# A two-layer scan kernel: old y added where y is copied out, and the second layer's preparation and stores spread over steps

## The chip, the cores and the metric

The kernel runs on one core of one Trainium2 chip. The metric is device time in microseconds (us) of one execution. Four engines compute: TensorE (PE: matrix products and transposes, into PSUM), VectorE (DVE), ScalarE (ACT) and GpSimd (POOL). SyncE (SP) issues most transfers, POOL issues those that add into memory. [...]

## The reference, cut to what matters

Two residual layers work on a picture of 4 batches x 64 x 64 positions x 192 channels. Each normalises its input, projects it to 384 inner channels and a gate, and runs a state-space scan with 16 states over the 4,096 positions in four directions: by rows, by columns, and both backwards. The four results are added, normalised, gated, and projected back.

```python
# first layer: a recurrence along L for each of 4 directions
dA = jnp.exp(dt[..., None] * A_k[None])
dBu = dt[..., None] * bt[:, :, None, :] * ut[..., None]
h = dA * h + dBu
y = jnp.einsum('bkdn,bkn->bkd', h, ct)
...
y = out_y[:, 0] + inv_y[:, 0] + wh_y + invwh_y
# second layer: the same kind of sum, by cumulative sums with a decay
log_decay = jnp.cumsum(log_dA, axis=1)
decay = jnp.exp(log_decay)
h = decay * jnp.cumsum(dB_u / (decay + 1e-12), axis=1)
y = jnp.einsum('bldn,bln->bld', h, C_mat)
```

In the second layer the decay dies out after a few positions for most states, so the kernel computes only the positions near the ends of each direction (and keeps a full version for data where that does not hold, behind a runtime test; it is not run on this data).

## The kernel before, in words

**First layer** (class FirstLayer, once per batch). `project` writes the transposed input uT, the skip term as the first value of y, and the B, C and dt rows to device memory. `scans` then works on 32 items, each one direction and 512 positions: items 0 to 15 go by rows (forward and backward in turn), 16 to 31 by columns. An item has 16 steps, one per state, numbered n; g numbers all 512 steps. In a step:

- ACT makes `xT` (L699, for step g+2) and the decay `a` (L711, for g+1);
- PE transposes xT into PSUM tiles `x` (L716, for g+1), of which there are three;
- DVE scans `h` along the positions in three pieces (L724) and keeps the last column (`carry`, L734);
- POOL multiplies `h` by the C row, broadcast over partitions by SP (`bct`, L704, L738);
- PE, at least three steps later (LAG = 3), transposes the product and adds it into three PSUM banks `yp` (`add_y`, L751).

The old y of the item's positions is loaded as `yold` (one SBUF buffer). PE puts it into `yp` by a product with the identity (`start_y`, L745) at steps 3 and 4, so that the sums begin from it; the item's own sums are added from step 4 on. `end_y` (L764) copies the banks to `yt` at steps 2 and 3 of the next item and SP stores it. For items that go the same way (rows or columns) as the one before, `yold` is loaded at step 5 of the item before. For item 16, the first by columns, it is loaded only after the last store by rows (L838).

Between these run the preparations of later items (`steps`, L668), each put at a step by hand: dt products on PE, Abs, Exp and Ln on ACT, four instructions on POOL, sums on DVE. The order on PE, ACT, DVE and POOL in this stage is the one written (a manual schedule); SP follows in the order of the program.

**Second layer** (class SecondLayer, all four batches in turn within each stage). `project`, then `prepare`, `scans` and `finish`. `prepare` takes two chunks per batch, main (M) and extension (E). For each it loads `uc`, makes the B, C and dt rows (`xp`, L1234), then in `delta` dt products (`dp`, L1160; three PSUM banks), Abs (L1167), Exp (L1168), four POOL instructions (L1171, L1172, L1173, L1175), Ln (L1174), the dt products once more and their use on DVE (L1177); then cumulative sums, a test, a product with uc (L1241), and in `keep` transposes and five stores. This part has no order written by hand: the framework's planner orders each engine's instructions by what is ready and by their place in the program.

`scans` of the second layer is written by hand again, with 9 steps per batch: four on M, two on a half-width chunk (two states each), one on E, two on a quarter-width chunk (four states each). For each step ACT makes a weight `sg` and a decay `a` (L1296), one step ahead; for the steps with four states POOL first multiplies (L1285) and ACT then takes one function of the whole (L1291). DVE multiplies and scans (L1344, L989), POOL multiplies by C (L1360), PE adds up two steps later (L1378). Results go to memory through transfers that add (`store`, L1407), issued by POOL: per batch six for the E result `yte` and six for the sum `ytm`, all six in a row. `store` takes four blocks; the first and third are one transfer each (L1412), the second and fourth two (L1415).

Of the kernel before, what the change touches and what calls it, by code (L numbers as in the profile page):

```python
# [10 lines left out]
F32 = mybir.dt.float32  # L11
# [6 lines left out]
ND = DI // 128  # L18
# [384 lines left out]
class FirstLayer:  # L403
# [151 lines left out]
    def scans(self):  # L555
        nc, tc = self.tc.nc, self.tc
        with ExitStack() as ctx:
# [181 lines left out]

            def start_y(it, b):  # L740

                if b == 0:
                    it.yp = [ps_y.tile([128, LC], F32, name=f"yp{i}") for i in range(ND)]
                yo = it.yold.rearrange("p j e -> p (j e)")[:, b * LC : (b + 1) * LC]
                nc.tensor.matmul(it.yp[b], ident, yo, start=True, stop=False, skip_group_check=True)  # L745

            def add_y(g, b):
                it, n = flat[g]
                for i in range(NJ):
                    j, d = divmod(b * NJ + i, ND)  # L750
                    nc.tensor.matmul(  # L751
                        it.yp[b][:, i * 128 : (i + 1) * 128],
                        hs[g][:, d, j * 128 : (j + 1) * 128],
                        ident,
                        start=False,
                        stop=n == NS - 1,
                        is_transpose=True,
                        skip_group_check=True,
                    )
# [21 lines left out]
            with tc.manual_schedule(engines={nc.tensor.engine, nc.scalar.engine, nc.vector.engine, nc.gpsimd.engine}):  # L781
# [17 lines left out]

                items[0].yold = load("yold", self.y_dram, items[0].k, items[0].c)  # L800
                c_rows(0)
# [7 lines left out]
                for g in range(N + LAG + 1):  # L809
# [10 lines left out]
                    adds = [[] for _ in range(ND)]  # L820
                    if it is not None:
                        for at, b in (((LAG, 1), 0), ((LAG, 2), 1), ((LAG + 1, 0), 2)):
                            if at[0] == n:
                                adds[at[1]].append((start_y, it, b))

# [4 lines left out]
                    for d in range(ND):  # L830
# [12 lines left out]
                    if g < N:  # L843
# [148 lines left out]
class SecondLayer(FirstLayer):  # L992
# [149 lines left out]
    def prepare(self, ucs, batches):  # L1142
        nc, tc = self.tc.nc, self.tc
        with ExitStack() as ctx:
# [17 lines left out]

            def delta(xd):

                e = p3.tile([128, ND, LC], F32, name="e")
                for d in range(ND):
# [8 lines left out]
                nc.gpsimd.tensor_tensor(e, e, wl, ALU.add)  # L1175
                for d in range(ND):
                    nc.vector.scalar_tensor_tensor(dt[:, d, :], dt_rows(xd, d), 0.0, e[:, d, :], ALU.max, ALU.add)  # L1177
                return dt, e

# [46 lines left out]

            for uc_dram, (main, ext, _, _) in zip(ucs, batches):
                before = None
                for r, chunk in enumerate((main, ext)):
                    uc = p2.tile([128, ND, LC], F32, name="uc")  # L1230
                    nc.sync.dma_start(uc, uc_dram[:, r])
                    xp = ps_x.tile([NX, LC], F32, name="xp")
                    for d in range(ND):
                        nc.tensor.matmul(xp, self.w_xp[:, d, 0, :], uc[:, d, :], start=(d == 0), stop=(d == ND - 1))  # L1234
                    xd = p2.tile([NX, LC], F32, name="xd")
                    nc.scalar.activation(xd, xp, AF.Identity, bias=self.xbias)
                    dt, e = delta(xd)
                    cum = sums(dt, before)
                    before = cum
                    test(cum, r)  # L1240
                    nc.vector.tensor_mul(e, dt, uc)  # L1241
                    if r == 0:
                        for at in (0, SEG, 3 * SEG - 1, 4 * SEG - 1):
                            nc.vector.memset(dt[:, :, at : at + 1], 1e30)
                    keep(chunk, xd, dt, cum, e)


    def scans(self, batches, ys):
        nc, tc = self.tc.nc, self.tc
        with ExitStack() as ctx:  # L1250
            pool = lambda name, bufs, **k: ctx.enter_context(tc.tile_pool(name=name, bufs=bufs, **k))
            p1, p2, p3, p5 = (pool(f"s{b}", b) for b in (1, 2, 3, 5))
            ps_y = pool("psy", 1, space=bass.MemoryType.PSUM)
# [134 lines left out]
            def ext_y(g, b):  # L1388
# [8 lines left out]
                if b == ND - 1:  # L1397
                    store(it.y, flat[g][2], SEG)

            def end_y(b):  # L1400
                y = p1.tile([128, NJ, DI], F32, name="ytm")
                for i in range(ND):
                    to = y.rearrange("p j e -> p (j e)")[:, i * LC : (i + 1) * LC]
                    (nc.scalar.copy if i == 1 else nc.vector.tensor_copy)(to, yp[i])
                store(y, b, 0)

            def store(y, b, near):  # L1407
                far = near + SEG
                v = ys[b].rearrange("(h w) e -> w h e", w=HW)
                for k, lo in enumerate((near, near, L - far, L - far)):  # L1410
                    if k % 2 == 0:
                        nc.gpsimd.dma_start(ys[b][lo : lo + SEG, :], y[:, k, :], accum_op=ALU.add)  # L1412
                        continue
                    for s in range(2):
                        nc.gpsimd.dma_start(v[lo // HW + s], y[s * HW : (s + 1) * HW, k, :], accum_op=ALU.add)  # L1415

            with tc.manual_schedule(engines={nc.tensor.engine, nc.scalar.engine, nc.vector.engine, nc.gpsimd.engine}):
# [12 lines left out]
                for g in range(N + LAG + 1):  # L1430
# [30 lines left out]

# [127 lines left out]
```

## Time and profile before

| | us |
|---|---|
| median of 3 runs | 11277.36 |
| lowest to highest of them | 11272.01 to 11278.86 |
| the profiled execution's own time | 11280.24 |
| its span, first to last instruction | 11278.4 |

| engine | busy us | share of the span |
|---|---|---|
| PE | 9593.1 | 85% |
| DVE | 9659.2 | 86% |
| ACT | 9787.2 | 87% |
| POOL | 8583.8 | 76% |

The first layer's scans fill most of the span: about 200 to 2400 us for the first batch, and the same again from about 2670, 5140 and 7610 us. The second layer starts at about 9810 us; its preparation lies between 10456 and 10656 us, its scans between 10673 and 11024, its last stage after that.

Times inside the profile are us from the start of the span. A row of the groups gives line, engine, operation, output and inputs with their shapes, the count, and then the busy time with the mean ns of one, and the idle time just before with what ended it. A row of the waits gives who waited for whom, the total in us, how often, and the longest. A row of windows gives from:to and length in us, then for PE, its weight loads, DVE, ACT and POOL the busy us (and number of instructions), the granted TensorE clock as a share of full speed, the DMA share and GB/s. A row of the timeline gives start, length, engine, line and operation, and in brackets the idle time before it with what ended it. In shapes, f32 is 4 bytes; one fp32 product shows as two matmuls.

### The profile page before, as it was taken

The page shows a single profiled execution, that of the slowest core. Times are in us where ns is not written, and L with a number is a line of the kernel's source. Part 1 is how long each engine was busy: PE and PEld are TensorE (multiplying, and loading weights), DVE is VectorE, ACT ScalarE, POOL GpSimd, SP SyncE. Part 2 cuts the span into 40 slices and gives each one's busy share as a digit, 9 for nine tenths or more (in the row PEclk, how much of TensorE's full clock was granted, in tenths as well). Part 3 has the DMA queues.
Part 4 walks back from the last instruction along what each step waited for, and adds up shares of the span by engine and source line. Part 5 has one row for each costly group of instructions (what it writes and reads, how often), then busy time and mean ns, then how long its engine had stood idle before and what let it go on. Part 6 is the DMA issues. An engine that isn't in the chain of part 4 may idle for free. (4 is left out here: it accounts for less than half of the span.)

```text
span 11278.4 us, 171696 instructions
## 1 busy us (share of the span) xinstructions
PE 9593.1 (85%) x61449; PEld 7301.6 (65%) x61449; DVE 9659.2 (86%) x11524; ACT 9787.2 (87%) x16986; POOL 8583.8 (76%) x2776
## 2 busy tenths in 40 slices
PE   7998888878988888888988888879988888788667
PEld 4776666655776666656766666647766666655356
DVE  4999899976999899957999899939998999888465
ACT  5999999977999999958999999949999999856567
POOL 3999899945999899928999899909998999700360
PEclk8999999988999999988999999979999999989688
DMA  4333333444333333344333334343333333434448
GB/s 124 109 105 98 94 98 100 97 133 125 109 104 99 94 99 98 97 149 112 111 100 96 96 98 98 89 164 107 109 100 94 98 98 98 127 114 128 159 104 272
DMA packets 831026, 1269.85 MB, mean 113 GB/s; under 512 B 99002, under 2 KB 514631, under 8 KB 829652
## 3 DMA queue, kind: packets, MB, share of 16 engines
q1 hardware_dynamic: 825300, 1252.49, 39.6%
q0 software_dynamic: 4864, 6.29, 0.4%
q8 instruction: 488, 8.00, 0.3%
q14 instruction: 374, 3.06, 0.1%
HBM read 958.19 MB, written 300.42 MB: 112 GB/s over the span
## 5 line engine op out<-in xcount | busy, mean ns | idle before, releaser
L738 POOL TENSOR_TENSOR h<-h,bct 128x1536 f32<-128x1536 f32 x2048 | 7062.4, 3469 | 591.4 <-DVE carry L734 487.9
L724 DVE TENSOR_TENSOR_SCAN h<-a,carry,x 128x512 f32<-128x512 f32 x5376 | 6607.0, 1267 | 238.7 <-PE x L716 191.7
L716 PE MATMUL x<-ident,xT 128*128 128x128 f32 x24576 | 4002.0, 287 | 817.7 <-DVE h L724 715.7
L699 ACT ACTIVATE xT<-dtuT,bT 128x384 f32<-128x384 f32 x8192 | 4358.6, 609 | 94.8 <-PE x L716 90.1
L716 PEld LDWEIGHTS x<-ident,xT 128*128 128x128 f32 x24576 | 2805.6, 145 | 2142.7 <-DVE h L724 925.7
L711 ACT ACTIVATE a<-dt,A_log_f 128x512 f32<-128x512 f32 x6144 | 3977.5, 716 | 0.0
L751 PE MATMUL yp<-ident,h 128*128 128x128 f32 x24576 | 3705.5, 277 | 9.2 <-POOL h L738 9.2
L751 PEld LDWEIGHTS yp<-ident,h 128*128 128x128 f32 x24576 | 2946.5, 144 | 78.8 <-issue 64.1
L615 PE MATMUL dp<-xd,w_dtb_f 13*128 13x512 f32 x1536 | 886.9, 661 | 213.6 <-DVE dt L644 212.0
L724 DVE TENSOR_TENSOR_SCAN h<-a,x 128x512 f32<-128x512 f32 x768 | 899.1, 1207 | 190.0 <-PE x L716 115.7
L628 POOL TENSOR_SCALAR wl<-e 128x1536 f32<-128x1536 f32 x128 | 189.1, 1478 | 919.6 <-ACT e L624 919.6
L490 PE MATMUL pp<-xT,w_in 96*128 96x512 f32 x1152 | 535.3, 615 | 0.0
L615 PEld LDWEIGHTS dp<-xd,w_dtb_f 13*128 13x128 f32 x1536 | 237.3, 190 | 457.0 <-DVE dt L644 341.2
L745 PE MATMUL yp<-yold,ident 128*128 128x512 f32 x768 | 444.1, 663 | 73.4 <-DMA yold<-y 73.4
L621 ACT ACTIVATE e<-dp 128x512 f32<-128x512 f32 x384 | 224.8, 585 | 311.9 <-DVE dt L644 161.7
L1106 DVE SCALAR_TENSOR_TENSOR acc<-pad,conv_w_s,acc 128x2048 f32<-128x2048 f32 x192 | 439.3, 2341 | 50.0 <-ACT acc L1104 49.4
L641 POOL TENSOR_TENSOR e<-e,wl 128x1536 f32<-128x1536 f32 x128 | 444.8, 3475 | 0.3
L1087 POOL MEMSET pad<- 128x66 f32 x12 | 1.9, 159 | 581.1 <-DVE acc L1106 456.0
L638 POOL TENSOR_TENSOR e<-e,dt 128x1536 f32<-128x1536 f32 x128 | 442.5, 3457 | 0.3
L490 PEld LDWEIGHTS pp<-xT,w_in 96*128 96x128 f32 x1152 | 221.5, 198 | 252.6 <-issue 243.5
L734 DVE TENSOR_REDUCE carry<-h 128x3 f32<-128x3 f32 x2048 | 322.7, 158 | 70.5
L644 DVE SCALAR_TENSOR_TENSOR dt<-dp,e 128x512 f32<-128x512 f32 x384 | 255.6, 666 | 74.6 <-POOL e L641 68.1
(172 smaller groups left out, 6855.1 us busy)
## 6 DMA issues: line engine op xcount, KB each, us to landing
bct<-xp SPq DMA_DIRECT2D x1024, 512.0 KB, 4.9
uT<-uT SPq DMA_DIRECT2D x64, 768.0 KB, 4.8
yold<-y SPq DMA_DIRECT2D x64, 768.0 KB, 7.9
y<-yt SPq DMA_DIRECT2D x64, 768.0 KB, 4.5
uT<-uT SPq DMA_DIRECT2D x128, 384.0 KB, 5.0
yold<-y SPq DMA_DIRECT2D x128, 384.0 KB, 5.4
y<-yt SPq DMA_DIRECT2D x128, 384.0 KB, 4.6
yt<-y SPq DMA_DIRECT2D x64, 768.0 KB, 10.8
```

The lines of the kernel that those rows point to most:

```text
L490: self.tc.nc.tensor.matmul(pp, self.w_in[:, i, e * 128 : (e + 1) * 128], self.xT[:, i, t * LC : (t + 1) * LC], start=(i == 0), stop=(i == ...
L615: nc.tensor.matmul(self.dp[d], w, self.xd[0 : DR + 1, :], start=True, stop=True)
L638: nc.gpsimd.tensor_tensor(self.e, self.e, self.dt, ALU.subtract)
L641: nc.gpsimd.tensor_tensor(self.e, self.e, self.wl, ALU.add)
L699: nc.scalar.mul(xTs[g][:, j, :], it.dtuT[:, j * DI : (j + 1) * DI], it.bT[:, j, n : n + 1])
L711: nc.scalar.activation(as_[g][:, d, :], it.dt[:, d, :], AF.Exp, scale=scale)
L716: nc.tensor.transpose(xs[g, d][:, j * 128 : (j + 1) * 128], xTs[g][:, j, d * 128 : (d + 1) * 128], ident)
L724: nc.vector.tensor_tensor_scan(along(hs[g][:, d, :], it.k), along(as_[g][:, d, :], it.k), along(xs.pop((g, d)), it.k), 0.0 if it.first els ...
L738: nc.gpsimd.tensor_tensor(hs[g], hs[g], bc(cs[g - n % 2][:, n % 2, :], 1, ND), ALU.mult)
L745: nc.tensor.matmul(it.yp[b], ident, yo, start=True, stop=False, skip_group_check=True)
L751: nc.tensor.matmul(it.yp[b][:, i * 128 : (i + 1) * 128], hs[g][:, d, j * 128 : (j + 1) * 128], ident, start=False, stop=n == NS - 1, is_tr ...
L1106: nc.vector.scalar_tensor_tensor(acc, part(tap), weight(tap), acc, ALU.mult, ALU.add)
```

## The change

In the first layer the identity products are gone: the first transposed product of an item starts each PSUM bank instead, and `end_y` adds `yold` on DVE in place of the copy. `yold` is loaded for every item alike, at step 8 of the item itself. In the second layer's `prepare` the work of a chunk up to Ln and the POOL instructions becomes `start`, called one chunk ahead of the rest. In its `scans` the weights and decays of the four-state steps are made two steps ahead (with a fourth buffer for `sg` and `a`), and the stores go on a list from which two are issued in each step, before the step's product on POOL.

```diff
-            def start_y(it, b):
-                if b == 0:
-                    it.yp = [ps_y.tile([128, LC], F32, name=f"yp{i}") for i in range(ND)]
-                yo = it.yold.rearrange("p j e -> p (j e)")[:, b * LC : (b + 1) * LC]
-                nc.tensor.matmul(it.yp[b], ident, yo, start=True, stop=False, skip_group_check=True)
             def add_y(g, b):
                 it, n = flat[g]
+                if n == 0 and b == 0:
+                    it.yp = [ps_y.tile([128, LC], F32, name=f"yp{i}") for i in range(ND)]
...
-                        start=False,
+                        start=n == 0 and i == 0,
...
             def end_y(it, b):
...
-                nc.vector.tensor_copy(it.yt.rearrange("p j e -> p (j e)")[:, b * LC : (b + 1) * LC], it.yp[b])
+                part = slice(b * LC, (b + 1) * LC)
+                yt, yo = (t.rearrange("p j e -> p (j e)")[:, part] for t in (it.yt, it.yold))
+                nc.vector.tensor_add(yt, it.yp[b], yo)
...
-                items[0].yold = load("yold", self.y_dram, items[0].k, items[0].c)
...
-                            if (n, d) == (LAG, 1) and it is not None and it.yold is None:
-                                it.yold = load("yold", self.y_dram, it.k, it.c)
...
-                        if n == 5 and i + 1 < len(items) and items[i + 1].k % 2 == it.k % 2:
-                            q = items[i + 1]
-                            q.yold = load("yold", self.y_dram, q.k, q.c)
+                        if n == 8:
+                            it.yold = load("yold", self.y_dram, it.k, it.c)
...
-            def delta(xd):
+            def start(uc_dram, r):
+                uc = p3.tile([128, ND, LC], F32, name="uc")
+                nc.sync.dma_start(uc, uc_dram[:, r])
+                xp = ps_x.tile([NX, LC], F32, name="xp")
+                for d in range(ND):
+                    nc.tensor.matmul(xp, self.w_xp[:, d, 0, :], uc[:, d, :], start=(d == 0), stop=(d == ND - 1))
+                xd = p3.tile([NX, LC], F32, name="xd")
+                nc.scalar.activation(xd, xp, AF.Identity, bias=self.xbias)
                 e = p3.tile([128, ND, LC], F32, name="e")
                 for d in range(ND):
                     nc.scalar.activation(e[:, d, :], dt_rows(xd, d), AF.Abs)
...
                 nc.gpsimd.tensor_tensor(e, e, wl, ALU.add)
-                for d in range(ND):
-                    nc.vector.scalar_tensor_tensor(dt[:, d, :], dt_rows(xd, d), 0.0, e[:, d, :], ALU.max, ALU.add)
-                return dt, e
+                return uc, xd, e, dt
...
+            order = [(b, r) for b in range(len(batches)) for r in range(2)]
+            ready = [start(ucs[b], r) for b, r in order[:1]]
+            for i, (b, r) in enumerate(order):
+                if i + 1 < len(order):
+                    ready.append(start(ucs[order[i + 1][0]], order[i + 1][1]))
+                uc, xd, e, dt = ready.pop(0)
+                for d in range(ND):
+                    nc.vector.scalar_tensor_tensor(dt[:, d, :], dt_rows(xd, d), 0.0, e[:, d, :], ALU.max, ALU.add)
+                before = cum = sums(dt, before if r else None)
+                nc.vector.tensor_mul(e, dt, uc)
+                test(cum, r)
...
+                keep(batches[b][r], xd, dt, cum, e)
...
-                sg[g] = p3.tile([128, ND, LC], F32, name="sg")
+                sg[g] = p4.tile([128, ND, LC], F32, name="sg")
...
-                as_[g] = p3.tile([128, ND, LC], F32, name="a")
+                as_[g] = p4.tile([128, ND, LC], F32, name="a")
...
-                    store(it.y, flat[g][2], SEG)
+                    stores.extend(store(it.y, flat[g][2], SEG))
...
-                store(y, b, 0)
+                stores.extend(store(y, b, 0))
...
+            def store_next():
+                to, of = stores.pop(0)
+                nc.gpsimd.dma_start(to, of, accum_op=ALU.add)
...
-                    if g + 1 < N:
-                        weight(g + 1)
-                        decay(g + 1)
+                    for q in (g + 1, g + 2):
+                        if q < N and (q - g == 2) == (len(flat[q][1]) == 4):
+                            weight(q)
+                            decay(q)
...
                             turn_x(g + 1, d)
+                        if d > 0 and stores:
+                            store_next()
...
+                while stores:
+                    store_next()
```

More of the change, by code (lines that the diff above doesn't have):

```diff
@@ L820, in scans @@
                     adds = [[] for _ in range(ND)]
[L821 to L824, printed above, removed]
                     ready = [x for x in late if x <= g - LAG and (n > LAG or x // NS < i)][:2]
@@ L1225, in keep @@
                 nc.sync.dma_start(chunk.dram["cum"], cum)
[L1227 to L1245, printed above, removed]
+            order = [(b, r) for b in range(len(batches)) for r in range(2)]
[9 more added lines that the diff above has]
+                test(cum, r)
+                if r == 0:
+                    for at in (0, SEG, 3 * SEG - 1, 4 * SEG - 1):
+                        nc.vector.memset(dt[:, :, at : at + 1], 1e30)
+                keep(batches[b][r], xd, dt, cum, e)
     def scans(self, batches, ys):
@@ L1251, in scans @@
             pool = lambda name, bufs, **k: ctx.enter_context(tc.tile_pool(name=name, bufs=bufs, **k))
-            p1, p2, p3, p5 = (pool(f"s{b}", b) for b in (1, 2, 3, 5))
+            p1, p2, p3, p4, p5 = (pool(f"s{b}", b) for b in (1, 2, 3, 4, 5))
             ps_y = pool("psy", 1, space=bass.MemoryType.PSUM)
@@ L1404, in end_y @@
                     (nc.scalar.copy if i == 1 else nc.vector.tensor_copy)(to, yp[i])
-                store(y, b, 0)
+                stores.extend(store(y, b, 0))
+            stores = []
             def store(y, b, near):
@@ L1409, in store @@
                 v = ys[b].rearrange("(h w) e -> w h e", w=HW)
+                r = []
                 for k, lo in enumerate((near, near, L - far, L - far)):
                     if k % 2 == 0:
[L1412 to L1415, printed above, removed]
+                        r.append((ys[b][lo : lo + SEG, :], y[:, k, :]))
+                    else:
+                        r += [(v[lo // HW + s], y[s * HW : (s + 1) * HW, k, :]) for s in range(2)]
+                return r
+            def store_next():
+                to, of = stores.pop(0)
+                nc.gpsimd.dma_start(to, of, accum_op=ALU.add)
             with tc.manual_schedule(engines={nc.tensor.engine, nc.scalar.engine, nc.vector.engine, nc.gpsimd.engine}):
```

## The prediction, made before the changed kernel was run

> **What bounds the kernel now.** I read the page's groups first, then the table of waits, then stretches of the timeline. In the first layer's scans (four batches of about 2,198 us each, 8,790 of the 11,278.4 us span) three engines are level:
>
> ```profile
> L738 POOL TENSOR_TENSOR h<-h,bct 128x1536 f32<-128x1536 f32 x2048 | 7062.4, 3469 | 591.4 <-DVE carry L734 487.9
> L724 DVE TENSOR_TENSOR_SCAN h<-a,carry,x 128x512 f32<-128x512 f32 x5376 | 6607.0, 1267 | 238.7 <-PE x L716 191.7
> L699 ACT ACTIVATE xT<-dtuT,bT 128x384 f32<-128x384 f32 x8192 | 4358.6, 609 | 94.8 <-PE x L716 90.1
> L711 ACT ACTIVATE a<-dt,A_log_f 128x512 f32<-128x512 f32 x6144 | 3977.5, 716 | 0.0
> L745 PE MATMUL yp<-yold,ident 128*128 128x512 f32 x768 | 444.1, 663 | 73.4 <-DMA yold<-y 73.4
> ```
>
> The means overlap their neighbours; from start to next start in the timeline an xT takes 0.506 us, an `a` 0.613, a scan 1.18. An item (16 steps, about 68 us) so costs ACT 16 x (4 x 0.506 + 3 x 0.613) = 61.8 plus 4.2 for Abs, Exp and Ln = 66.0; POOL 16 x 3.47 + 9.9 = 65.4; DVE about 64. PE issues 24 transposes a step at 0.109: 41.9 plus about 14 of other products, so it has room. One place stands out in the waits, and a window over it (1311 to 1326) shows everything still, beside a normal one:
>
> ```profile
> PE yp L745 <- DMA yold<-y: 73.4, 4, 18.6
> 3400.00:3600.00 200.00, 175.05 (x1215) 137.25 (x1214) 192.38 (x218) 194.04 (x344) 189.78 (x59) 0.97 0.36 99
> 1311.00:1326.00 15.00, 2.76 (x7) 1.65 (x8) 0.00 (x0) 0.00 (x0) 1.94 (x1) 0.50 0.48 87
> ```
>
> This is item 16, the first by columns: its old y can only be loaded once item 15 is stored (step 3), and the identity product needs it at step 3. It comes once per batch; that item takes 84.9 to 86.5 us, its neighbours 66 to 69.
>
> The second layer's preparation (8 chunks, 10456 to 10656) alternates. POOL's timeline, and PE's beside it:
>
> ```profile
> 10481.36 3.41 POOL L1175 TENSOR_TENSOR e<-e,wl 128x1536 f32<-128x1536 f32 x1
> 10494.55 1.47 POOL L1171 TENSOR_SCALAR wl<-e 128x1536 f32<-128x1536 f32 x1 [9.78 <-ACT e L1168]
> 10501.17 3.42 POOL L1175 TENSOR_TENSOR e<-e,wl 128x1536 f32<-128x1536 f32 x1
> 10512.42 1.69 POOL L1171 TENSOR_SCALAR wl<-e 128x1536 f32<-128x1536 f32 x1 [7.83 <-ACT e L1168]
> ...
> 10485.55 7.19 PE L1160 MATMUL dp<-xd,w_dtb_s 13*128 13x512 f32 x8 [11.33 <-DVE dt L1177]
> ```
>
> PE's second dt products of a chunk hold the three banks until DVE's L1177 has used them, and the next chunk's first products wait behind: POOL ends (L1175) come 151.5 us / 7 = 21.65 us apart, though POOL needs 9.9 per chunk.
>
> The second layer's scans run 66.0 us for batch 0, then 82.5, 85.3 and 80.4 (first L1344 of each). POOL's queue shows why, with DVE's timeline last:
>
> ```profile
> 10742.75 0.90 POOL L1412 DMA_DIRECT2D y<-yte  x1 [2.54 <-ACT xT L1326]
> 10746.67 1.68 POOL L1415 DMA_DIRECT2D y<-yte  x2 [3.02 <-DMA y<-yte]
> 10747.79 10.78 POOL L1360 TENSOR_TENSOR h<-h,bct 128x1536 f32<-128x1536 f32 x3
> ...
> 10756.34 0.70 DVE L1344 SCALAR_TENSOR_TENSOR x<-sg,x 128x512 f32<-128x512 f32 x1 [9.21 <-PE x L1337]
> ```
>
> Six stores in a row each wait for the last landing; three products pile up behind; PE waits for them and DVE for PE.
>
> [...] the copy yt<-yp averages 675 ns, the two-operand dtuT<-tp,uT (L664) 674. [...] here they land after 3.1 to 3.8 us (96 and 192 KB), so I use those and the gaps.
>
> **The change, part by part.** All sums against the profiled execution's own 11,280.2 us (span 11,278.4), which is 2.9 above the median of the runs, 11,277.4.
>
> *L745 removed.* Per item 6 passes x 0.431 = 2.6 us of PE, 331 us over 128 items. They lie in steps 3 and 4, which take 5.53 and 3.77 us: three scans and a carry (3.77), in step 3 with the three copies of 0.582. DVE sets them, so this PE time is hidden: 0.
>
> *Copy becomes add.* 384 times; L664, the same shape with one PSUM operand, has the same 0.582 pitch: 0. It now waits on a DMA semaphore too. [...] A gain is excluded, there is no less work. If an add cost double, 384 x 0.58 = 223 us more on a nearly full engine.
>
> *yold load moved* to step 8 of its own item. Same DMAs (one, or two by columns). On SP it stands behind the C rows for step 10, which wait for the product of step 5; behind it queue the next C rows and uT. The load lands in 5.7 us (median; most 9.6). Its first reader is at step 2 of the next item, ten steps or some 42 us later; item i-1's store is five steps (21 us) old. Cost 0; with that cover gone 5.7 to 9.6 per item. The initial load goes too: 0, it stood beside other loads.
>
> *The stall goes.* ACT idles 16.2 us and DVE 17.9 in it. Next late is ACT, at 66.0 per item against 85.7: at most 19.7. ACT's own idle says 16 to 17.3. I take 17.5 x 4 = **70** (64 to 78).
>
> *Preparation as a pipeline.* The next chunk's loads, dt products, Abs, Exp, POOL work and Ln are issued ahead of this chunk's second products. No arithmetic is added. POOL (9.9), ACT (10.3: 82.3 / 8, table loads in it) and DVE (9.1) leave PE as the floor: 129.35 / 8 = 16.2 us busy at a granted clock of 0.63. At full clock a pass takes 0.43 instead of 0.85, so about 10. I take 16, since the clock is likely to rise a little: 7 x (21.65 - 16) = **40**. Ends: 0 if the order on PE comes out as before (this part has no hand-written order: the trace already runs B transposes, written last, ahead of second products), 75 at a pitch of 11.
>
> *Stores spread, 4-state weights a step earlier.* Batch 0 has no stores; its losses are ACT and DVE waits on POOL's L1285 at the last two steps. One step ahead removes them: 66.0 to 58 (ACT is busy 57.85). For batches 1 to 3 POOL's queue decides: 9 products x 3.45 = 31.1, two L1285 sets x 6.2 = 12.4, 12 stores x 0.9 = 10.8. Two stores go in a step, in the order block 0, block 1's halves, block 2, block 3's halves. In the first two pairs the second must wait for the first to land, in the third not; nine such gaps in the trace average 3.6. So 4 x 3.6 = 14.4; sum 68.7. A product behind them comes up to some 8 us late by step 4, and about 16 with the L1285 sets at 5 and 6, while PE's slack is about 9: DVE follows POOL, 69.5 with the catching up. Before 314.2, after 58 + 3 x 69.5 = 266.5: **48**. Ends: 15 (gaps of 4.8, and PE blocked as before), 74 (POOL keeps ahead, 61 per batch, just over ACT). The tail keeps its twelve serial stores: 0.
>
> Finish and projection are untouched. Sum 70 + 40 + 48 = 158: 11,280.2 - 158 = 11,122, less 2.9: **11,119 us**.
>
> **Rivals.**
> *A. Preparation stays serial.* The order there makes second products first again; for it speak the hoisted transposes, against it that the next chunk's first products now stand ahead in the program. 70 + 5 + 48 = 123: 11,154.
> *B. The spread stores block POOL as before.* For: every store still waits for the one before. Against: a product lies between pairs. 70 + 40 + 12 = 122: 11,155.
> *C. Everything overlaps.* PE's clock rises, POOL is never late: 78 + 70 + 72 = 220: 11,057.
> *D. The add costs more than the copy* (the slower side). Place: L764, 384 times on DVE, 96% busy in its stage. It decides at 158 / 384 = 0.41 us more each, 0.99 instead of 0.58; at double, 11,119 + 223 = 11,342. L664 speaks against it.
> *E. No net change*, gains eaten by such costs: within 0.2%.
>
> **How the numbers follow.** Forecast 0.55, A 0.17, B 0.12, C 0.09, D 0.05, E 0.02. The forecast's own range is 11,085 to 11,150. Adding A and B to it, and going part of the way to C, gives 11,060 to 11,175, which leaves out D, E and half of C. About 0.2% (22 us) is what a measurement can tell: faster 0.93, same 0.02, slower 0.05.
>
> **What would show it.** Right: no wait for yold in the waits, item 16 near 67 us, yt an add near 675 ns; POOL ends in preparation 16 us apart; L1344 batch starts some 58 and 70 us apart. Wrong: the yt group well above 675 ns or waiting on yold; PE idle before dp still 11 us; POOL products in threes behind stores.

## The result, and the profile after

| | before | after |
|---|---|---|
| median of 4 runs, us | 11,278.11 | 11,207.92 |
| lowest to highest | 11,272.01 to 11,280.64 | 11,201.71 to 11,214.49 |
| ratio, 95% interval | | 0.9939 (0.9921 to 0.9956) |
| the profiled execution's own time | 11,280.24 | 11,207.48 |
| its span | 11,278.4 | 11,205.6 |
| mean granted TensorE clock over the span | 0.932 | 0.913 |

Faster, as forecast, but by 70 us where 158 were forecast. The forecast was 11,119 and its range ended at 11,175. The groups of the changed kernel, from the page (the add's row from the full list of groups):

```profile
L738 POOL TENSOR_TENSOR h<-h,bct 128x1536 f32<-128x1536 f32 x2048 | 7065.7, 3474 | 559.3 <-DVE carry L734 512.8
L724 DVE TENSOR_TENSOR_SCAN h<-a,carry,x 128x512 f32<-128x512 f32 x5376 | 6614.9, 1266 | 282.0 <-PE x L716 231.5
L699 ACT ACTIVATE xT<-dtuT,bT 128x384 f32<-128x384 f32 x8192 | 4355.6, 608 | 40.4 <-PE x L716 34.6
L761 DVE TENSOR_TENSOR yt<-yp,yold 128x512 f32<-128x512 f32 x384 | 258.5, 674 | 21.9 <-PE yp L746 18.0 <-issue 1.0
```

L745 has gone and nothing waits for `yold`. The add takes 674 ns where the copy took 675, so this part did what it says and cost nothing. But VectorE's idle time before its scans, which held the 73 us stall before, rose from 238.7 to 282.0 us, and the part that PE's `x` ends went from 191.7 to 231.5. Where the stall stood, and in the window shown before, the windows now read:

```profile
1311.00:1326.00 15.00, 13.73 (x88) 12.37 (x88) 13.58 (x16) 15.00 (x29) 15.00 (x6) 0.77 0.66 147
3400.00:3600.00 200.00, 173.22 (x1202) 140.00 (x1200) 191.35 (x217) 193.71 (x344) 189.42 (x60) 0.94 0.36 100
```

The standstill is gone: ACT and POOL are busy all of the 15 us. In the second row one number has moved in the wrong direction, TensorE's granted clock: 0.97 before, 0.94 now, in a stretch with no stall in either.

Read from first and last instructions, the difference of 72.8 us between the two spans splits so (us):

| stretch | before | after | difference | forecast |
|---|---|---|---|---|
| start to the last carry of the first layer | 9,794.9 | 9,755.0 | -39.9 | -70 |
| from there to the first `xd` of the second layer's preparation | 663.5 | 681.2 | +17.7 | 0 |
| first `xd` to the last `dtuT` copy | 189.1 | 184.7 | -4.4 | -40 |
| from there to the end (scans, last stage) | 630.9 | 584.7 | -46.2 | -48 |

Two parts of three gave less than forecast, and one stretch that the prediction had no term for grew. The third part came out as forecast. POOL's timeline in the second layer's scans shows it: a product after every two stores, where before six stores stood in a row and three products behind them.

```profile
10702.44 1.05 POOL L1413 DMA_DIRECT2D y<-yte  x1
10706.76 0.84 POOL L1413 DMA_DIRECT2D y<-yte  x1 [3.26 <-DMA y<-yte]
10707.34 3.74 POOL L1350 TENSOR_TENSOR h<-h,bct 128x1536 f32<-128x1536 f32 x1
```

The wait for the store before is still there (3.26 us here), as the sum assumed. Batches start 58.9, 69.7 and 72.7 us apart and the last takes about 69, where 58 and three times 69.5 were forecast.

In the preparation, POOL's timeline is now this, and PE's groups (window of the preparation) follow, first before, then after:

```profile
10456.58 3.67 POOL L1169 TENSOR_TENSOR e<-e,dt 128x1536 f32<-128x1536 f32 x1
10463.16 4.93 POOL L1171 TENSOR_TENSOR e<-e,wl 128x1536 f32<-128x1536 f32 x1 [2.91 <-ACT wl L1170]
...
10496.03 1.47 POOL L1167 TENSOR_SCALAR wl<-e 128x1536 f32<-128x1536 f32 x1 [17.93 <-ACT e L1164]
```

```profile
L1160 PE MATMUL dp<-xd,w_dtb_s 13*128 13x512 f32 x96 | 70.3, 888 | 22.2 <-DVE dt L1177 22.1
...
L1221 PE MATMUL tp<-ident,e 128*128 128x128 f32 x96 | 23.0, 426 | 31.4 <-DVE end L1203 17.5 <-DVE dt L1244 13.4 <-DVE e L1241 0.5
```

```profile
L1149 PE MATMUL dp<-xd,w_dtb_s 13*128 13x512 f32 x96 | 72.4, 921 | 2.7 <-ACT e L1163 1.4 <-ACT xd L1160 1.1 <-DVE dt L1228 0.2
...
L1215 PE MATMUL tp<-ident,e 128*128 128x128 f32 x96 | 22.7, 424 | 55.4 <-DVE end L1197 48.9 <-DVE e L1230 6.4
```

PE's waits ahead of `dp`, 22.2 us in total before (11.33 in the line that the prediction showed), are down to 2.7. Yet POOL's last instructions of each chunk are still 21.7 us apart in the mean (14.8, 10.0, 28.5, 26.8, 23.1, 25.3, 23.6), because PE now waits elsewhere: 55.4 us at the transposes `tp`, for VectorE, where the kernel before had 31.4.

### The profile page after: what moved, and what is told of

It reads as the page before. It is cut to its first block, busy times and chain, and to the rows that moved or that the text cites. A ratio compares the mean times of both kernels' runs of the same rounds, so it can differ in the third digit from the quotient of the medians.

```text
span 11205.6 us, 170040 instructions
## 1 busy us (share of the span) xinstructions
PE 9475.0 (85%) x60681; PEld 7392.8 (66%) x60681; DVE 9717.1 (87%) x11524; ACT 9789.6 (87%) x16986; POOL 8587.6 (77%) x2776
## 5 line engine op out<-in xcount | busy, mean ns | idle before, releaser
L724 DVE TENSOR_TENSOR_SCAN h<-a,carry,x 128x512 f32<-128x512 f32 x5376 | 6614.9, 1266 | 282.0 <-PE x L716 231.5
L716 PE MATMUL x<-ident,xT 128*128 128x128 f32 x24576 | 4116.1, 293 | 986.8 <-DVE h L724 885.7
L716 PEld LDWEIGHTS x<-ident,xT 128*128 128x128 f32 x24576 | 2889.2, 148 | 2172.4 <-DVE h L724 1011.7
L746 PE MATMUL yp<-ident,h 128*128 128x128 f32 x24576 | 3846.2, 285 | 9.2 <-POOL h L738 9.2
L746 PEld LDWEIGHTS yp<-ident,h 128*128 128x128 f32 x24576 | 3084.1, 149 | 11.1 <-POOL h L738 11.1
L890 PE MATMUL vp<-ident,yt 128*128 128x128 f32 x768 | 139.5, 331 | 197.4 <-ACT yt L885 185.6
```

Source lines behind the costliest of these rows:

```text
L716: nc.tensor.transpose(xs[g, d][:, j * 128 : (j + 1) * 128], xTs[g][:, j, d * 128 : (d + 1) * 128], ident)
L724: nc.vector.tensor_tensor_scan(along(hs[g][:, d, :], it.k), along(as_[g][:, d, :], it.k), along(xs.pop((g, d)), it.k), 0.0 if it.first els ...
L746: nc.tensor.matmul(it.yp[b][:, i * 128 : (i + 1) * 128], hs[g][:, d, j * 128 : (j + 1) * 128], ident, start=n == 0 and i == 0, stop=n == N ...
```

## The experiments

Three questions: which part gave what; what the first layer gave back; what became of the preparation. The kernels that were timed together share their runs of the kernel before (median 11,275.97 for l1_alone, prep_alone, scans_alone and zero3; 11,275.79 for zero3_late, psum_keep, zero3_8_9 and zero3_oldprep; 11,281.97 for zero3_psum and zero5_psum; 11,275.0 for the two kernels with uc_two in their name; 11,279.82 for the two with uc_own). Ratios are to that, with 95% intervals.

### Each part alone

l1_alone is the kernel before with the first layer's edits only, prep_alone with `start` and the loop in `prepare` only, scans_alone with the second layer's stores and weights only.

> The first layer's part of the change on the kernel before, nothing else. The profile after says that item 16 lost its stall (4 x 19 us) and that the other items grew, so that the four scan stages together fell by 31 us and their heads by some 8. Theory (TensorE's granted clock falls to half more often without the wide products): about 11,240 us against 11,278, and a mean granted clock in the scan stages of about 0.94 instead of 0.97. The forecast on record for this part: 11,208.

> The preparation's part alone on the kernel before. Theory (VectorE and GpSimd now work at the same time and block one another, what is gained by overlap is lost): within 8 us of 11,278, DVE busy in the preparation near 120 us instead of 73. The forecast on record for this part: 11,238. If something else in the changed kernel (its other parts) held the preparation up, this run alone would show the 40 us.

> The part in the second layer's scans alone (spread stores, four-state weights a step earlier) on the kernel before. By the step starts in the profile after: 314 us falls to about 270, so 11,234 us; batches of 59, 70, 73 and 69 us. If the parts depend on one another, another number.

| | median us | ratio (95%) |
|---|---|---|
| l1_alone | 11,246.27 | 0.9975 (0.9964 to 0.9986) |
| prep_alone | 11,288.69 | 1.0012 (1.0004 to 1.0020) |
| scans_alone | 11,240.82 | 0.9967 (0.9954 to 0.9979) |

The new preparation by itself makes the kernel 13 us slower. The first layer's part gives 30 us, not 70, with nothing else changed, and the scans 35. The parts alone add up to 52 us; together they gave 70 of this measurement. That gap is no larger than the uncertainty of three differences, and is not explained further.

### The first layer: what the identity products did besides

The four scan stages (first to last carry of a batch) together took 8,791.5 us before and 8,760.2 after, 31.2 less. Item 16 went from 84.9 to 86.5 us down to 66.0 to 66.5, so the stall gave about 4 x 19.4 = 78 us, more than forecast. The other 31 items of each batch therefore lost some 47 us. Counting a step from one `carry` to the next, some 28 of these are at step 5, whose median grew from 3.77 us to between 3.83 and 4.12 in the four batches; most of the rest is at steps 9 and 11. One item in which it is large (item 20 of the second batch, step 5 in 5.28 us), in PE's timeline, with one instruction of VectorE's after it:

```profile
4040.12 0.63 PE L716 MATMUL x<-ident,xT 128*128 128x128 f32 x4 [1.14 <-DVE h L724]
4041.89 0.63 PE L716 MATMUL x<-ident,xT 128*128 128x128 f32 x4 [1.14 <-DVE h L724]
4043.22 1.12 PE L716 MATMUL x<-ident,xT 128*128 128x128 f32 x4 [0.70 <-DVE h L724]
4044.13 1.92 PE L746 MATMUL yp<-ident,h 128*128 128x128 f32 x8
...
4049.50 1.28 DVE L724 TENSOR_TENSOR_SCAN h<-a,carry,x 128x512 f32<-128x512 f32 x1 [1.22 <-PE x L716]
```

and the windows over the two stretches:

```profile
4036.10:4042.40 6.30, 2.86 (x20) 2.11 (x20) 6.20 (x9) 6.30 (x13) 6.30 (x3) 1.00 0.46 91
4042.40:4049.20 6.80, 6.10 (x30) 5.99 (x29) 5.77 (x6) 5.66 (x10) 6.80 (x3) 0.50 0.38 109
```

In step 3 PE has three groups of four transposes and no more; the three adds hold up VectorE's scans, PE waits for VectorE and is busy 2.86 of 6.30 us. Then the clock stands at 0.50 for 6.8 us, and that is just when PE gets the items' own sums to catch up with: the same four transposes take 1.12 us instead of 0.63. PE comes late, and VectorE waits 1.22 us for `x`. In the same item of the kernel before, the identity products (1.02 us each) start at 4064.06, 4065.83 and 4067.19 us: PE is busy 3.84 of the 6.30 us from 4059.7 and all of the 6.80 after, and the clock is 1.00 in both.

PE's longest pause in this stretch is 1.14 us. That such pauses bring the clock down was the author's theory; one item does not show it. Stretches at half clock in the records of the scan stages, all multiples of 3.413 us (after the change 152 of one such length, 67 of two and one of three):

| | number | total us | four stages, us |
|---|---|---|---|
| before | 133 | 553 | 8,791.5 |
| after | 220 | 986 | 8,760.2 |
| l1_alone | 222 | 990 | 8,757.2 |
| scans_alone | 132 | 543 | 8,791.2 |

To test the theory, zero3 gives PE something to do at the places of the old products without bringing `yold` back: a product of the identity with zeros opens each bank.

```diff
+            zero = p1.tile([128, LC // 2], F32, name="zero")       # set to 0.0 once
+            def zero_y(it, b, start):
+                nc.tensor.matmul(it.yp[b].rearrange("p (a w) -> p a w", a=2), ident, bc(zero, 1, 2), start=start, stop=False, skip_group_check=True)
...
-                        start=n == 0 and i == 0,
+                        start=False,
...
+                        for at, b, start in [((3, 1), 0, True), ((3, 2), 1, True), ((4, 0), 2, True)]:
+                            if at[0] == n:
+                                adds[at[1]].append((zero_y, it, b, start))
```

> The changed kernel with three products of the identity with zeros per item put where the identity products stood (steps 3, 3 and 4); they open the PSUM banks, the add on VectorE and the late load stay. It adds 2.6 us of TensorE work per item. Clock theory: half-clock spells in the scans go back from about 220 to about 130, steps 4 and 5 to 3.77 us, and the 48 us that the other items lost come back: about 11,163 us. Rival (the items grew because of the add, its second wait, or where the load now stands): no gain, 11,208 or, with more TensorE work, slower.

Measured 11,164.61, ratio 0.9898 (0.9883 to 0.9913): 43 us faster than the changed kernel, by doing more on PE. The add on VectorE and the late load are still in it, so the loss is not theirs. Its stages take 8,705.5 us (54.7 less than after), with 129 stretches and 468 us at half clock. The stage row, and PE's timeline at step 3:

```profile
3400.00:3600.00 200.00, 174.97 (x1218) 137.32 (x1217) 191.83 (x217) 194.36 (x344) 188.90 (x59) 0.97 0.34 100
```

```profile
4020.23 1.02 PE L746 MATMUL yp<-zero,ident 128*128 128x512 f32 x2
4021.54 0.63 PE L719 MATMUL x<-ident,xT 128*128 128x128 f32 x4 [0.28 <-DVE h L727]
4022.00 1.02 PE L746 MATMUL yp<-zero,ident 128*128 128x512 f32 x2
...
4024.22 1.04 PE L752 MATMUL yp<-ident,h 128*128 128x128 f32 x8
```

The clock is back at 0.97, and the eight transposes of `h` that took 1.92 us take 1.04. The waits of VectorE's scan for `x` fall from 259.4 to 234.4 us.

In zero3 a product opens each bank, in the changed kernel a transpose, so the opening could be a rival cause. The trace of the kernel before, where products open every bank, shows what the loss goes with. In 89 of 120 items (the first and item 16 of each batch left out) no half-clock stretch touches steps 4 and 5, and step 5 takes 3.59 to 3.77 us. In the other 31 one does, and step 5 takes 4.22 to 5.87 us. After the change all 120 items have such a stretch, in zero3 24. So in the kernel before the loss came without a transpose that opens a bank; whether one adds to it was not varied by itself. Nor did transposes as such go with half the clock: from 4068.1 to 4074.1 us before, PE does nothing else, is busy all 6.00 us, and the clock is 1.00.

A control, zero3_late: the same three products, but at step 14, where they can't help step 4 (banks opened as in the changed kernel).

```diff
+   [((14, 0), 0, False), ((14, 1), 1, False), ((14, 2), 2, False)]
```

> The changed kernel with the same three products with zeros per item, but at step 14, where TensorE is not behind: the control for the run with them at steps 3 and 4. They add zeros to banks already open. Clock theory: the half-clock spells at steps 3 and 4 stay (about 220 in the scans), the time stays at 11,208 us, or up to 10 us more. Rival (more TensorE work anywhere, or wide products as such, raise the clock): towards 11,165 us.

Measured 11,294.74, ratio 1.0016 (1.0009 to 1.0023): 87 us slower than the changed kernel and 77 outside the expectation. The part that it was for came out: the half-clock stretches stay (221, 973 us, where zero3 has 129 and 468), so with the same number of products it was their place that made the difference. The cost was not foreseen. It lies in items 0 to 7, in which step 15 takes 4.46 us instead of 3.77 and the next step 0 takes 5.83 instead of 3.94: about 2.6 us x 8 items x 4 batches = 84. In these items PE also works on the gate at steps 13 to 15. That leaves some 3 of the 87 us to the 96 later items. Here the filler was free in steps 3 and 4, where PE waited, and not beside the gate's products.

Of the stretches that remain in zero3, most lie at steps 9 and 10, as in the kernel before. zero3_8_9 puts two more zero products there.

```diff
+   ((8, 1), 0, False), ((9, 1), 1, False)
```

> The run with three zero products at steps 3 and 4, with two more at steps 8 and 9, where the profile still shows 0.45 and 0.31 half-clock windows per item. Clock theory: these spells go too, and with them a part of what steps 9 to 11 take over 4.36, 3.77 and 4.36 us (4.9, 4.9 and 4.8): about 11,130 us against 11,164. Rival (steps 9 to 11 wait for VectorE to free a bank, not for a slow TensorE): no gain or, with 1.7 us more TensorE work per item there, up to 20 us slower.

Measured 11,195.99, ratio 0.9933 (0.9919 to 0.9946), so 31 us slower than zero3. The stretches did fall (83, 287 us) but the stages rose to 8,733.3. In the mean step 11 went from 4.82 to 5.15 us and step 9 from 4.93 to 5.07, more than step 10 gave back (4.81 to 4.54). So the clock's share alone is no goal: with 181 us less at half clock the stages took 27.8 us more.

### The preparation: VectorE's sums take longer beside GpSimd

The preparation does the same arithmetic in both kernels, but the cumulative sums (24 and 48 instructions in the window of the preparation) take longer. From the groups, before, after, and in psum_keep:

```profile
L989 DVE TENSOR_TENSOR_SCAN cum<-one,cum,dt 128x128 f32<-128x128 f32 x48 | 18.4, 458 | 0.0
L989 DVE TENSOR_TENSOR_SCAN cum<-keep_s,dt 128x256 f32<-128x256 f32 x24 | 14.4, 666 | 0.0
```

```profile
L978 DVE TENSOR_TENSOR_SCAN cum<-keep_s,dt 128x256 f32<-128x256 f32 x24 | 40.1, 1723 | 0.1
L978 DVE TENSOR_TENSOR_SCAN cum<-one,cum,dt 128x128 f32<-128x128 f32 x48 | 35.6, 807 | 0.1
```

```profile
L978 DVE TENSOR_TENSOR_SCAN cum<-keep_p,cum,dt 128x128 f32<-128x128 f32 x48 | 18.6, 461 | 0.1
L978 DVE TENSOR_TENSOR_SCAN cum<-keep_p,dt 128x256 f32<-128x256 f32 x24 | 14.7, 669 | 0.1
```

Before, VectorE and POOL worked mostly in turn; in the pipeline they work at once. The two sums with `keep` and `dt`, both in SBUF, went from 32.8 us to 75.7. In the trace after, 13 of the 24 longer sums (128x256) have no POOL instruction beside them and take 0.66 to 0.69 us; the 11 that have one take 1.31 to 3.85. The one of 3.85 us runs from 10456.95 to 10460.80, POOL's L1169 above from 10456.58 to 10460.25. POOL's L1171 of 4.93 us (3.42 before) stands beside a test product of 3.41 us (0.15 alone). VectorE's busy time in the preparation went from 73.0 to 119.9 us. `dt`, from a PSUM and an SBUF operand (L1228), takes 686 ns in the mean (684 before), and the 15 of 24 beside a POOL instruction 671 to 693. That the place of the operands makes this difference was the author's theory, and psum_keep tests it: the constant operand goes to PSUM, the arithmetic stays.

```diff
-            ps_t = pool("pst", 3, space=bass.MemoryType.PSUM)
+            ps_t = pool("pst", 2, space=bass.MemoryType.PSUM)
+            keep_p = pool("pk", 1, space=bass.MemoryType.PSUM).tile([128, LC], F32, name="keep_p")
+            nc.vector.tensor_copy(keep_p, self.keep)
...
-                            scan_add(nc, cum[:, d, part], self.keep[:, part], dt[:, d, part], 0.0, k == 1)
+                            scan_add(nc, cum[:, d, part], keep_p[:, part], dt[:, d, part], 0.0, k == 1)
...
-                            one = self.one.to_broadcast([128, SEG])
+                            one = keep_p[:, 1:2].to_broadcast([128, SEG])
```

> The changed kernel, where in the preparation the constant operand of the cumulative sums (the ones that are 0 at the segment starts, and the plain ones) stands in PSUM instead of SBUF; one transpose buffer in PSUM pays for it. The sums then read one SBUF operand. Theory (VectorE's instructions with two SBUF operands wait for GpSimd's): none of the sums takes over 1 us, DVE busy in the preparation falls from 120 to about 90 us, and with it some 25 us of the time: 11,183. Rival (the order on TensorE alone, transposes ahead of the next chunk's products, holds the pitch): DVE busy falls, the time does not, 11,208.

Measured 11,171.99, ratio 0.9909 (0.9894 to 0.9924): 36 us faster than the changed kernel. The sums are back at 33.3 us (third fence); six of the longer ones take 3.58 us together from 10467.51, while POOL works on L1170 (1.47 us) and L1171 (3.42). PE's wait at `tp` falls from 55.4 to 19.4 us, the preparation takes 147.6 us instead of 184.7, and POOL's last instructions are 16.6 us apart, where the prediction had put 16. VectorE is still busy 93.5 us, because other instructions with two SBUF inputs now take longer: `e = dt*uc` 18.9 us instead of 13.8, the test products 22.9 instead of 7.9. POOL's last instruction of a chunk still takes 4.49 us in the mean (3.42 before, 3.71 after).

zero3_oldprep is zero3 with `prepare` as before the change, to see what the new one is worth there.

> Three zero products at steps 3 and 4, with the preparation of the kernel before. If the preparation's part costs what it cost alone (13 us), 11,152 us against 11,164.

Measured 11,153.51, ratio 0.9895 (0.9880 to 0.9911): 11 us faster than zero3. Without the PSUM operand the new preparation costs, with it, it pays. Both findings together are zero3_psum, and zero5_psum has five zero products, all in step 3, so that PE has little idle time there:

```diff
+   [((3, 0), 0, True), ((3, 1), 0, True), ((3, 1), 1, True), ((3, 2), 1, True), ((3, 2), 2, True)]
```

> Both remedies on the changed kernel: three zero products at steps 3 and 4, and the constant operand of the preparation's sums in PSUM. If the two losses are independent, 11,208 - 43 - 36 = 11,129 us.

> The same with five zero products, all in step 3 (twice into two of the banks, once into the third), none in step 4. Clock theory: the spells still seen at step 3 (0.2 to 0.3 windows per item with three products) go, and step 4, where TensorE catches up, has less to do: 0 to 15 us faster than with three. Rival (the remaining spells cost nothing, as those at steps 8 and 9 did): the same within 10 us.

zero3_psum took 11,128.40 (0.9866, 0.9849 to 0.9882): the two gains add up. zero5_psum took 11,125.44 (0.9861, 0.9845 to 0.9878), the same within the uncertainty, though the half-clock stretches fell further, from 128 (464 us) to 107 (379 us).

### The late start of the preparation

In all kernels so far with the new preparation the first `xd` comes 681 to 688 us after the first layer's last carry, with the old one 664 to 666. PE's timeline at that place, after:

```profile
10415.43 5.32 PE L1113 MATMUL dq<-dg_s,u 128*128 128x128 f32 x32 [2.75 <-ACT u L1096]
10431.17 5.79 PE L1158 MATMUL xp<-uc,w_xq_s 128*64 128x512 f32 x8 [10.41 <-DMA uc<-uc]
```

and SyncE's waits over 10415 to 10450:

```profile
SPq L1155 <- DMA y<-du: 1.9, 2, 1.2
```

The first `xp` waits 10.41 us for the load of `uc`. SyncE issues that load only at 10426.04, after the last transfers `y<-du`, the end of the projection, and its wait for them. Before, the load waited for a product of the projection instead (first line below; the second is uc_two's), was issued at 10448.56, 13.8 us ahead of the projection's last copy of `du` (10462.31), and was hidden.

```profile
SPq L1231 <- PE pp L490: 2.3, 1, 2.3
SPq L1155 <- PE pp L490: 2.3, 1, 2.3
```

The change has moved `uc` and `xd` from the pool of two buffers to the pool of three; that this pool lies where the projection's `du` still is was the theory. uc_two puts them back; it can't tell place from number of buffers, so uc_own gives them a pool of three of their own, ahead of the others. Both edits in short:

```diff
-                uc = p3.tile(...)        xd = p3.tile(...)
+                uc = p2.tile(...)        xd = p2.tile(...)        # uc_two
+                uc = p0.tile(...)        xd = p0.tile(...)        # uc_own, with p0 = pool("q0", 3) opened first
```

> The changed kernel with one thing undone in the second layer's preparation: uc and xd lie again in the pool of two buffers, as before the change, instead of the pool of three. In the traces the first xd of the preparation comes 664 to 666 us after the last carry of the first layer with the old preparation and 681 to 688 with the new one, where the first load of uc waits for a transfer y<-du of the projection. Theory: that wait comes from where the three-buffer pool lies (over the projection's du), so here the first xd comes at 663 to 667 again, 15 to 18 us earlier, and the run takes 11,191 us (11,186 to 11,197) where the changed kernel takes 11,208. Rival 1, the late start comes from the order of the program (start is called ahead of the loop): first xd still at 681 or later, time within 5 us of 11,208. Rival 2, two buffers of uc and xd hold up the pipeline: first xd early, but the preparation longer by more than 10 us.

> The fastest version so far (five zero products in step 3, the constant operand of the cumulative sums in PSUM; 11,125 us) with uc and xd in the pool of two buffers. Theory: the first xd comes 20 us earlier (686.5 us after the last carry, 664 to 667 expected), and since the preparation now has little slack in it most of that reaches the end: 11,107 us (11,102 to 11,114). Rival, the start is early but the two buffers lengthen the preparation from 146 us to 160 or more: 11,120 to 11,130.

> The changed kernel with uc and xd in a pool of three buffers of their own, opened ahead of the other two, so that they lie where uc lay before the change. Theory (place decides the start, three buffers keep the pipeline): first xd 661 to 667 us after the last carry instead of 681, preparation 185 us as in the changed kernel, 15 to 18 us faster than it: 11,191 us (11,184 to 11,198). Rival 1 (three buffers ahead of the others still reach over a buffer of the projection): first xd at 675 or later, 11,203 to 11,213. Rival 2 (the early start is given back in the preparation, which waits for what ends the projection or for its own exclusion of VectorE and GpSimd): first xd early, preparation 195 us or more, 11,200 to 11,210.

> The fastest version so far (11,125 us) with the same three-buffer pool for uc and xd. Theory: first xd at 662 to 667 us after the last carry instead of 686.5, preparation 146 to 150 us, so 11,105 us (11,100 to 11,112). Rivals as for the run beside it: 11,118 to 11,128 if the place does not help or the early start is given back.

| | last carry to first `xd` | preparation | median us | ratio (95%) |
|---|---|---|---|---|
| after | 681.2 | 184.7 | 11,207.92 | 0.9939 (0.9921 to 0.9956) |
| uc_two | 661.6 | 241.4 | 11,252.30 | 0.9982 (0.9975 to 0.9988) |
| uc_own | 664.8 | 189.4 | 11,204.23 | 0.9937 (0.9920 to 0.9953) |
| zero5_psum | 686.5 | 146.0 | 11,125.44 | 0.9861 (0.9845 to 0.9878) |
| zero5_psum_uc_two | 665.6 | 202.1 | 11,159.26 | 0.9897 (0.9882 to 0.9912) |
| zero5_psum_uc_own | 667.0 | 158.6 | 11,119.96 | 0.9862 (0.9846 to 0.9879) |

The place decides the start: in both pools that lie first, it is 16 to 21 us earlier. The number of buffers decides the pipeline: with two of `uc` and `xd`, the preparation is 56 to 57 us longer, one chunk every 32 us in uc_two and every 25 in the other, and the runs are 44 and 34 us slower, the opposite of the theory. With three in the right place the preparation starts early, but is 4.7 and 12.6 us longer, so 11.7 and 6.9 us remain in the profiles. In the runs the gain is 4 and 5 us, which these intervals can't tell from nothing. The expected 15 to 20 us did not reach the end; the rival, that the early start is given back, was nearer. Some 8 us of the early start go in the first chunk: from the first `xd` to POOL's first instruction it takes 15 us in the two kernels with uc_own and 7 in after and zero5_psum. The projection's last `du` copies still run then, until 670 to 672 us after the last carry; that they are the reason was not tested. zero5_psum_uc_own and zero5_psum are the fastest versions, about 1.4% below the kernel before, and can't be told apart.

## Why the prediction was right or wrong

**The stall goes: right, a little small.** 19.4 us per batch where 17.5 was taken (limits 16 and 19.5).

**"L745 removed ... this PE time is hidden: 0": the step that failed in the first layer.** The time was hidden, as the sum said. But the products also kept PE occupied in step 3 (in the item shown 3.84 of 6.30 us, after the change 2.86). Without them TensorE's clock was granted at half about twice as long (986 us for 553), and the steps after lost 47 us. Three products with zeros brought 54.7 us back in the stages; the same three elsewhere brought none. That the clock is the way from the one to the other rests on the transposes that take nearly twice as long (1.12 us for 0.63), and on step 5, which before the change grew in the 31 items with a half-clock stretch (4.22 to 5.87 us) and in none of the 89 others (3.59 to 3.77).

**The copy becomes an add, and the load moves: right, 0 and 0.** 674 ns against 675, no wait for `yold`. Rival D, the slower one, fell.

**"Preparation as a pipeline ... DVE (9.1) leave PE as the floor": the step that failed there.** VectorE's 9.1 us per chunk was read from a trace in which POOL mostly stood still meanwhile (both were busy in 8.3 us of the window, after in 71.6); side by side with POOL it was 15.0 (119.9 / 8). The pitch of 16 was right only once the sums had one operand in PSUM: 16.6. The trace of before held a hint that was passed over: at 10598 to 10603 us, where POOL ran beside VectorE, a test product (L1203) took 1.45 us where the shortest took 0.13, a maximum of 128x1 (L1206) 1.31 for 0.15, and POOL's L1171 2.39 for 1.47. Rival A named nearly this outcome for the part (5 us gained, 4.4 measured), but for another reason: the order on PE. PE's wait ahead of `dp` was nearly gone, as the forecast had said, so its cause fell.

**A step that was missing: `uc` and `xd` in another pool.** "No arithmetic is added" passed over two words of the diff. The first load then waited for the projection's last stores, 17.7 us in the spans. With the 4.4 us gained after it, the preparation cost 13.3 instead of giving 40, and prep_alone's 13 us slower agrees. In the other traces with the same preparations this stretch takes 194 to 195 us with the old one and 183 to 187 with the new one, so its gain may be nearer to 10 than to 4.4.

**The stores spread: right, 48 forecast, 46 measured.** The prediction's 3.1 to 3.8 us to landing are those of POOL's transfers `y<-yte` and `y<-ytm` in the kernel before. The batches came as in the sum (58.9, then 69 to 73), and the second of two stores waited 3.2 to 4.7 us in most pairs, 6.7 in one (3.6 taken). Rival B fell.

**The sum.** 70 + 40 + 48 = 158 became 39.9 - 13.3 + 46.2 = 72.8 in the profiled execution (70 in the medians). Of the difference, 47 us went to the other items of the first layer, where the clock fell, 36 to VectorE's instructions beside POOL (psum_keep's gain), 18 to the late start and 2 to the scans' term; 8 more than forecast came from the stall, and 8 from the stretches between the batches, which the forecast left alone; in zero3, with the same edits, these are as long as before (813 and 812 us in all), so the 8 are no sure effect of the change. These are sizes from different kernels, so they add up only roughly. Rival C counted on a rising clock in the preparation; in its window it went from 0.62 to 0.59.

## What to carry to other kernels

Before counting the removal of hidden work as nothing, ask what it kept going: here, after three pauses of PE of 1.12 to 1.14 us within 6.30 us, the clock stood at 0.50 for 6.8 us, and three products of zeros made the kernel 43 us faster in steps 3 and 4, where PE waited, and 87 us slower at step 14. When two engines that worked in turn are made to overlap, look at where each instruction's operands lie: the sums with two SBUF inputs, 32.8 us in the serial version, took 75.7 once GpSimd worked beside them, and 33.3 with the constant operand in PSUM. A buffer moved to another pool can lie elsewhere in memory, and so inherit a wait from the stage before (here 17.7 us).

## What the runs showed of the hardware that was not expected

- After 6.30 us with PE busy for 2.86 and no pause above 1.14 us the clock fell to 0.50, for 6.83 us (two stretches of 3.413), and came back to 1.00 at 4049.2 us while PE did transposes alone. What decides it, these runs don't show: in the same stretch of the kernel before, with PE busy for 3.84 us and a longest pause of 1.14, the clock stayed at 1.00.
- Beside a POOL instruction a VectorE cumulative sum of 128x256 with two SBUF inputs took up to 3.85 us (0.66 to 0.69 alone), and a maximum of 128x1 up to 3.15 us (0.15 to 0.16 alone). With the constant operand in PSUM the sums took 0.67 us in the mean. A POOL product took up to 4.93 us instead of 3.42.
- More work on PE made the kernel 43 us faster; products of zeros took 1.02 us each time in steps 3 and 4, and those at step 14 cost 2.6 us per item in items 0 to 7, beside the gate's products.
